# A router product moved from the late turns of a fused two-layer kernel to its first layer, and kept in DRAM in between

## The chip, the core and the metric

The kernel runs on one core of one Trainium2 chip. The metric is the device time of one execution in microseconds (us); lower is better. The engines are named as the profile names them: PE (TensorE, the matrix unit, with PEld for its weight loads), DVE (VectorE), ACT (ScalarE), POOL (GpSimd) and SP (SyncE, which here only issues transfers). SP, ACT and POOL each have a queue of DMA transfers of their own, and all queues feed the same 16 DMA engines.

## What is computed

The input x is 8 sequences of 128 tokens of width 512, all float32. Layer 0 picks one 512x512 matrix for each sequence by an index, multiplies, and puts the result through a small mixture of low-rank experts; the result is added to x. Layer 1 is an attention with 32 query heads and 8 key/value heads over a paged cache of 512 positions and the 128 new ones, followed by a feed-forward part with a router. The change touches only the router of that last part:

```
q      = einsum('bsd,rd->bsr', y, Wq_w)      # Wq_w: 16 x 512
scores = einsum('bsr,er->bse', q, keys)      # keys: 64 x 16
top_w  = softmax(top 16 of 64 scores)
z      = einsum('bsd,nd->bsn', y, A_w)       # 512 -> 64 experts x 8
out    = einsum('bsn,on->bso', z * gate(top_w), B_w) * 2
```

Nothing stands between the two router products, so the kernel multiplies the two weights once, into a matrix of 512 x 64, and then multiplies each y by that matrix. The product of the two weights does not depend on x; it could be made at any time.

## The kernel before, in words

**Layer 0** is the loop at lines 711 to 780, one pass t for each of the 8 sequences. Pass t issues to PE the first half of the sequence's adapter product (`l0_adapter(t, True)`, line 621: 8 multiplications written as 16 instructions, since a float32 product takes two), then pieces of earlier sequences, then the second half (`l0_adapter(t, False)`), which ends with a copy of the result from PSUM to SBUF by ACT (line 630, tile cT). After that come the loads of later sequences on SP's queue, and `l0_base(t)`: the gate product from cT (line 638, tile cp) and the base product from cT and the base weights bww (line 643, tile bp). In pass 0 there is no other sequence to fill the time in which PE waits for the first cT. That is the first wait which the change names. Ahead of the loop PE does 32 transposes of an identity (line 710) while the first loads are under way.

The loads of the start are issued by three queues. ACT's queue has the first input tile and the gate weights. SP's queue has, in this order, the index list, the first sequence's matrix in four pieces of 256 KB (line 510), bww of 1 MB (line 538), the second sequence's input of 256 KB (line 503, tile xT), its matrix of 1 MB (line 510), and then smaller ones. POOL's queue has the norm weights nw (line 118), four pieces of a page list vpg (line 565), the lengths leni (line 579) and the rotation frequencies fr (line 581). POOL issues a transfer by an instruction that keeps it busy for about half a microsecond.

**Layer 1** is a loop of turns u = 1 to 66 (`iteration`), of which 64 are heads of the attention for one sequence. Order on every engine is the order in which the program is written; nothing reorders it later. In a turn PE does the four score products (lines 439 and 442), the output projection of an earlier turn (lines 1062 and 1075, tile y), projections for a later turn (line 265), and the value product (line 938, tile o). The constants read u = NU - 5 = 59 and u = NU - 7 = 57, with NU = 64.

In turn 57 the function `f_weights(0)` takes over a buffer that attention weights have left, and has POOL load the two router weights into it (`fw_t["r"]`, line 817, 16 rows of 2 KB, and `fw_t["k"]`, line 818, 16 rows of 256 bytes) and a part of the first feed-forward weight (line 822). In turn 59, between the second and the third score product, `f_fold` multiplies them: 4 multiplications of 16 x 128 by 16 x 64 (line 828, 8 instructions on PE, tile rk, which the profile calls fr; the frequencies of layer 0 have the same name there, on POOL), and a copy from PSUM into the buffer by DVE (line 831). From turn 59 on, once a turn, `f_project` (line 848) uses the product together with the feed-forward weight, as one matrix of 320 columns.

Two points of the machinery matter below. Each transfer on POOL's queue signals one of 8 semaphores in rotation, and an instruction that issues a transfer first waits until the previous transfer of the same semaphore has landed. And tiles of layer 0 borrow homes in buffers that layer 1 fills later: the matrices of sequences 5 to 7 lie in the first six of the seven slices of the buffer `wo_t`, and slice 6 is empty in layer 0 until `transpose_qk(2, wo_t[:, 6, ...])` writes it at the end of layer 0 (line 794).

Of the kernel before, what the change touches and what calls it, by code (L numbers as in the profile page):

```python
# [9 lines left out]
F32 = mybir.dt.float32  # L10
# [6 lines left out]
P = 128  # L17
B = 8
S = 128
DM = 512  # L20
NC = DM // P
# [18 lines left out]
E1, R1, RD = 64, 8, 16  # L40
# [18 lines left out]
def adaln_ffn_kernel(  # L59
# [25 lines left out]
    nc = tc.nc  # L85
# [33 lines left out]
        out=nw, in_=norm_w.rearrange("o (t d) -> o t d", t=2).to_broadcast([P, 2, D])  # L119
# [16 lines left out]
    yp = ctx.enter_context(tc.tile_pool(name="yp", bufs=2))  # L136
    dram = ctx.enter_context(tc.tile_pool(name="dram", bufs=1, space=bass.MemoryType.DRAM))
    y_d = [dram.tile([P, 4, HN], F32, name=f"yd_{b}") for b in range(B // 2)]
    x1_d = [dram.tile([P, DM], F32, name=f"x1d_{b}") for b in range(B)]
    ya_t, yp_t = {}, {}  # L140

# [7 lines left out]
    wo_t = wp.tile([P, 7, REP * HN], F32, tag="wo", name="wo")  # L149
# [67 lines left out]
    def bank(tag, name):  # L217
        return ps_1.tile([P, DM], F32, tag=tag, name=name)
# [3 lines left out]
    def banks(name, which=None):  # L222
        if which is None:
            which, turn_of[0] = turn_of[0], 1 - turn_of[0]
        return ps_s.tile([P, 2 * DM], F32, tag=f"s{which}", name=name)
# [267 lines left out]
    with ExitStack() as l0:  # L493
# [35 lines left out]
        for b in range(4):  # L529
            t = pairs[b // 2].rearrange("p x n -> p (x n)")[:, b % 2 * NC * DM :][:, : NC * DM]  # L530
            wt_home[b] = t.rearrange("p (o n) -> p o n", o=NC)
        for b in (5, 6, 7):
            t = wo_t[:, 2 * b - 10 : 2 * b - 8].rearrange("p x n -> p (x n)")
# [30 lines left out]
        for i in range(QD):  # L564
            nc.gpsimd.dma_start(
                out=vpg[i * 32 : (i + 1) * 32], in_=vpages[i : i + 1].to_broadcast([32, B * LC])
# [45 lines left out]
        def l0_adapter(b, first):  # L612

            xT, wt, xb = loaded[b]
            if first:
                cp_t[b] = banks(f"cp_{b}", 0)
                lg_t[b] = sm.tile([P, E0 + 8], F32, tag="lg", name=f"lg_{b}")
                nc.gpsimd.memset(lg_t[b][:, E0:], BIG)
            for o in range(0, NC // 2) if first else range(NC // 2, NC):
                for c in range(NC):  # L620
                    nc.tensor.matmul(  # L621
                        out=cp_t[b][:, o * S : (o + 1) * S],
                        lhsT=wt[:, o, c * P : (c + 1) * P],
                        rhs=xT[:, c, :],
                        start=(c == 0),
                        stop=(c == NC - 1),
                    )
            if not first:
                cT_t[b] = p2.tile([P, NC, S], F32, tag="cT", name=f"cT_{b}")
                nc.scalar.copy(cT_t[b].rearrange("p c s -> p (c s)"), cp_t[b][:, :DM])  # L630
# [74 lines left out]
            nc.scalar.copy(half.rearrange("p x c s -> p (x c s)"), tp[:, :DM])  # L705


        idle = bank("q", "idle")
        for i in range(WARM):
            nc.tensor.transpose(idle[:, :S], ident, ident)  # L710
        for t in range(B):
            l0_adapter(t, True)
            if t >= 1:
                l0_turn_low(t - 1)
            if t == 7:
                scores(0, 1, 1)
                mask_exp(0, 1)
                normalize(0, 0)
            l0_adapter(t, False)
            if t + 3 < B:  # L720
                l0_load(t + 3)
            if t + 2 < B:
                l0_load_x(t + 2)
            if t in (3, 4):
                load_q(t - 3)
            if 2 <= t <= 5:
                gather(0, (t - 2) * 4, (t - 1) * 4)
            elif t > 5:
                gather(1, (t - 6) * 8, (t - 5) * 8)
            if t >= 2:  # L730
                l0_turn(t - 2)
            if t == 4:
                project_whole(0, 0, 0, 1)
            if t == 5:
                norms(0)
                make_mask(0)
                project_whole(0, 1, 0, 1)
            if t == 6:
                transpose_qk(0)
                project_whole(0, 0, 1, 1)  # L740
            if t == 7:
                norms(2)
                project_whole(0, 1, 1, 1)
                transpose_qk(1)
            if t >= 1:
                l0_experts(t - 1)
            if t == 7:
                scores(0, 2, 1)
                mask_exp(0, 2)
                normalize(0, 1)  # L750
                new_pb(0)
                blocks(0, 0)
            l0_base(t)
            if t == 0:
                l0_rows()
            if 1 <= t <= 4:
                l0_angles(t - 1)
            if t in (3, 6):
                gather_v(t // 3 - 1, 0, LC)
            if t in (4, 5):  # L760
                make_tables(t - 4)
            if t == 4:
                project_whole(0, 0, 0, 0)
            if t == 5:
                project_whole(0, 1, 0, 0)
                norms(1)
                rotate(0)
                sums_q(nc.gpsimd, 0, 3, 2)
            if t == 6:
                scores(0, 0, 1)  # L770
                mask_exp(0, 0)
                project_whole(0, 0, 1, 0)
                rotate(1)
                sums_q(nc.gpsimd, 0, 4)
            if t == 7:
                scores(0, 3, 1)
                mask_exp(0, 3)
                normalize(0, 2)
                blocks(0, 1)
                project_whole(0, 1, 1, 0)  # L780
# [23 lines left out]
    fw_t, zg_t = {}, {}  # L804

    def f_weights(piece):

        if piece == 0:
            w = wp.tile([P, 7 * 2 * HW], F32, tag="wqkv", name="fw", bufs=GH)
            at = 0  # L810
            for n, rows, c in (("sa", P, NC), ("b", P, NC), ("r", RD, NC), ("k", RD, 1)):
                size = c * {"r": P, "k": E1, "sa": E1 + DM}.get(n, DM)
                fw_t[n] = w[:rows, at : at + size].rearrange("p (c n) -> p c n", c=c)
                at += size
            fw_t["k"] = fw_t["k"][:, 0]
            fw_t["s"], fw_t["a"] = fw_t["sa"][:, :, :E1], fw_t["sa"][:, :, E1:]
            nc.gpsimd.dma_start(out=fw_t["r"], in_=wr.rearrange("r (c p) -> r c p", p=P))
            nc.gpsimd.dma_start(out=fw_t["k"], in_=keys)
        n, c = ("a", piece) if piece < 2 else ("b", piece - 3)
        if piece != 2:  # L820
            src = (aw if n == "a" else bw).rearrange("(c p) n -> p c n", p=P)
            nc.gpsimd.dma_start(out=fw_t[n][:, 2 * c : 2 * c + 2], in_=src[:, 2 * c : 2 * c + 2])

    def f_fold(psum):

        rk = psum("r", [P, NC, E1])
        for c in range(NC):
            nc.tensor.matmul(
                out=rk[:, c, :], lhsT=fw_t["r"][:, c, :], rhs=fw_t["k"], start=True, stop=True
            )  # L830
        nc.vector.tensor_copy(fw_t["s"], rk)

    ORDER = (0, 1, 4, 2, 3, 5, 6, 7)

# [72 lines left out]
    with ExitStack() as l1:  # L907
# [336 lines left out]
        def iteration(u):  # L1244
# [3 lines left out]
            r, group = u % 16, (u // 16 + 1) * GH  # L1248
            f = room(fb) if fb is not None else None

            if u % 4 == 3:
                k, j, four = (u + 5) // 4, 0, True
            elif u % 4 == 0:
                k, j, four = (u + 4) // 4, 0, False
            elif u % 4 == 1:
                k, j, four = (u + 3) // 4, 1, True
            else:
                k, j, four = (u + 2) // 4, 1, False
# [30 lines left out]
            for h in range(REP):  # L1289
                if on(u):  # L1290
                    if (u, h) not in ((1, 0), (1, 1)):
                        scores(u, h)
                        mask_exp(u, h)
                    if h > 0 and (u, h) != (1, 1):
                        normalize(u, h - 1)

                    sums_o(u, h)
                    sums_w(u, h)
                    if 16 <= u < NU - 8 and (r, h) == (2, 3):
                        load_o(u // 16, (1, B12))  # L1300

                    if h == 2:
                        new_pb(u)
                        if u + 2 in range(3, NU):
                            blocks_qk(u + 2, u)
                    if h > 1:
                        blocks(u, h - 2)
                    if h == 1 and u == NU - 5:
                        f_fold(f[1])
                    if h == 3:  # L1310
                        z_blocks(u - NU + 4)
                    if h == (1 if u == NU - 3 else 2) and fb is not None:
                        yT_t[fb] = f_turn(fb, *f)
                if on(u - 3):
                    output(u - 3, h)
                    sums_a(u - 3, h)
                if h > 0 and slots:
                    project(k, j, slots[h - 1 : h])

                if (u, h) in WHOLE:  # L1320
                    project_whole(1, *WHOLE[u, h])
# [23 lines left out]
            if 16 <= u < NU - 8 and r in (0, 1, 2):  # L1345
                n = u // 16
# [184 lines left out]
```

## Time and profile before

| what | value |
|---|---|
| median of 3 runs | 1212.44 us (1210.85 to 1214.88) |
| profiled execution | 1214.63 us, its span 1211.9 us |
| PE busy | 1194.7 us, 99% of the span |
| DVE, POOL, ACT busy | 912.1, 741.2, 504.2 us |
| DMA over the span | 302.71 MB, mean 250 GB/s |
| granted TensorE clock | 1.000 over the span |

The busy time of PE is from the first to the modelled end of each instruction, so 99% says that PE almost never stands without work, not that it works at its peak. The profile's chain of waits is followed back from the last instruction: at each step it goes to what released it, or to the instruction ahead of it on its engine. A piece of work that lies in the chain moves the end if it grows or shrinks; one that does not lie in it moves the end only once it has used up its slack. The granted clock of a stretch is 1.000 when TensorE's clock was not throttled.

### The profile page before, as it was taken

To read this page: it belongs to the slowest core of one execution; us is meant where nothing else is said; L and a number is where in the kernel's file an instruction comes from. 1 tells how busy PE (TensorE), PEld (TensorE's weight loads), DVE (VectorE), ACT (ScalarE), POOL (GpSimd) and SP (SyncE) were. 2 spreads that over 40 slices of the span, in tenths; PEclk is the share of its full clock that TensorE was granted. 3 is DMA by queue.
4 is the path that set the end of the run, shared out by engine and by line. 5 is a ranking of instruction groups with operands and counts; after the bars stand their busy time and mean duration, and the time that the engine had idled before them with its cause. 6 is when DMAs were issued, how large, how long until landed. Compare 5 with 4: busy or idle time off the path is not lost.

```text
span 1211.9 us, 16793 instructions
## 1 busy us (share of the span) xinstructions
PE 1194.7 (99%) x4159; PEld 714.1 (59%) x4159; DVE 912.1 (75%) x2103; ACT 504.2 (42%) x1457; POOL 741.2 (61%) x826
## 2 busy tenths in 40 slices
PE   8999899999999999999999999999999999999998
PEld 6666455565555656555556555555656555565554
DVE  3547788877987887888887787878878888877632
ACT  1244554444444444444444444444444444443211
POOL 2444689778755677578756685687657684743100
PEclk9999999999999999999999999999999999999999
DMA  8823788888888988888889978897989888887742
GB/s 310 269 93 107 237 249 247 254 272 282 258 256 249 313 250 271 260 290 287 244 256 284 289 231 281 288 290 239 276 248 305 255 262 249 269 269 232 232 140 96
DMA packets 206260, 302.71 MB, mean 250 GB/s; under 512 B 84755, under 2 KB 119828, under 8 KB 205268
## 3 DMA queue, kind: packets, MB, share of 16 engines
q1 hardware_dynamic: 171220, 197.02, 53.4%
q10 hardware_dynamic: 18720, 52.49, 13.8%
q0 software_dynamic: 16224, 52.14, 12.5%
q8 instruction: 33, 0.54, 0.2%
q14 instruction: 63, 0.52, 0.1%
HBM read 185.64 MB, written 115.93 MB: 249 GB/s over the span
## 4 chain that ended last, share of the span: by engine, by line
PE 89%; DMA 5%; issue 1%; DVE 1%; POOL 1%; ACT 1%; ACTq 0%; SPq 0%; DVEq 0%; POOLq 0%
PE o L938 20%; PE p L265 19%; PE s L439 17%; PE y L1062 13%; PE s L442 4%; PE p L298 3%; DMA px<-pb 3%; PE y L1075 2%; PE bp L643 2%; PE op L1418 2%; PE cp L621 2%; PE fr L848 1%; PE fz L848 1%; DMA qkb<-px 1%; DMA bww<-in_base_w 1%
## 5 line engine op out<-in xcount | busy, mean ns | idle before, releaser
L463 ACT ACTIVATE p<-p,low 128x640 f32<-128x640 f32 x256 | 211.8, 827 | 438.3 <-DVE den L468 270.8
L469 POOL TENSOR_SCALAR p<-p,den 128x640 f32<-128x640 f32 x256 | 210.8, 824 | 230.1 <-DVE den L468 228.8
L452 DVE CUSTOM_DVE_ANT_0 p<-s,mask,rs 128x640 f32<-128x640 f32 x256 | 222.1, 878 | 80.7 <-PE s L442 80.0
L265 PE MATMUL p<-wqkv,xo 128*128 128x384 f32 x784 | 280.7, 486 | 0.4 <-POOL wqkv L166 0.3
L439 PE MATMUL s<-kt,qkT 128*128 128x512 f32 x504 | 258.4, 594 | 4.9 <-ACT oT L961 2.2
L938 PE MATMUL o<-pT,vt 128*128 128x512 f32 x512 | 230.2, 592 | 0.0
L474 DVE STREAM_TRANSPOSE pb<-p 128x640 f32<-128x640 f32 x252 | 208.0, 826 | 23.7 <-POOL p L469 23.7
L1062 PE MATMUL y<-wo,oT 128*128 128x256 f32 x784 | 206.4, 380 | 0.0
L265 PEld LDWEIGHTS p<-wqkv,xo 128*128 128x128 f32 x784 | 148.4, 190 | 69.1 <-POOL wqkv L166 1.2
L442 PEld LDWEIGHTS s<-qkT 128*128 128x128 f32 x504 | 95.8, 190 | 120.5 <-issue 120.5
L206 POOL DMA_INDIRECT vt<-in_vc,vrow x128 | 138.8, 1084 | 40.9 <-issue 31.1
L938 PEld LDWEIGHTS o<-pT,vt 128*128 128x128 f32 x512 | 97.2, 190 | 107.9 <-issue 92.8
L439 PEld LDWEIGHTS s<-kt,qkT 128*128 128x128 f32 x504 | 94.3, 190 | 77.8 <-issue 30.3
L1062 PEld LDWEIGHTS y<-wo,oT 128*128 128x128 f32 x784 | 131.8, 191 | 8.7
L314 ACT ACTIVATE sq<-c 128x128 f32<-128x128 f32 x320 | 98.8, 309 | 8.1
L442 PE MATMUL s<-qkT 128*128 128x128 f32 x504 | 96.8, 274 | 0.0
L320 POOL TENSOR_TENSOR rs<-ss,mhalf 128x5 f32<-128x5 f32 x64 | 83.1, 1299 | 5.3
L961 ACT COPY oT<-o 128x512 f32<-128x512 f32 x64 | 37.5, 585 | 100.7 <-PE o L938 73.0
L318 POOL TENSOR_SCALAR ss<-ss,eps 128x5 f32<-128x5 f32 x64 | 26.5, 414 | 77.4 <-ACT sq L314 77.3
L938 PE MATMUL o<-pT,vn 128*128 128x512 f32 x128 | 65.4, 592 | 0.0
L425 DVE STREAM_TRANSPOSE pb<-ca 128x640 f32<-128x640 f32 x61 | 50.9, 835 | 18.0 <-DMA kt<-in_kc 10.5
L268 DVE TENSOR_TENSOR c<-c,p 128x384 f32<-128x384 f32 x84 | 44.9, 534 | 21.7 <-PE p L265 21.4
(194 smaller groups left out, 1435.5 us busy)
## 6 DMA issues: line engine op xcount, KB each, us to landing
pT<-px SPq DMA_DIRECT2D x64, 1280.0 KB, 7.6
px<-pb SPq DMA_DIRECT2D x122, 400.0 KB, 5.4
px<-pb ACTq DMA_DIRECT2D x122, 400.0 KB, 5.6
qkb<-px SPq DMA_DIRECT2D x61, 320.0 KB, 4.3
kt<-in_kc SPq DMA_DIRECT2D x512, 32.0 KB, 4.9
wqkv<-in_wqkv POOLq DMA_DIRECT2D x32, 384.0 KB, 4.7
wo<-in_wo POOLq DMA_DIRECT2D x17, 512.0 KB, 8.1
yd<-yp POOLq DMA_DIRECT2D x12, 512.0 KB, 9.3
```

The source lines that it names most:

```text
L206: nc.gpsimd.indirect_dma_start(out=kv_t[step][1][:, c, :], out_offset=None, in_=vc, in_offset=bass.IndirectOffsetOnAxis(ap=vrow[:, hf, at ...
L265: nc.tensor.matmul(out=ps, lhsT=xo[:, pr, x, c, :], rhs=w[:, c, :], start=(c == 0), stop=(c == 1))
L314: nc.scalar.activation(sq, cs[:, at : at + D], AF.Square, accum_out=ss[:, h : h + 1])
L320: nc.gpsimd.tensor_tensor(rs, ss, mhalf, ALU.pow)
L439: nc.tensor.matmul(out=s[:, :L], lhsT=qkT[:, h, :], rhs=kt[:, :, g % GH, :], start=True, stop=True)
L442: nc.tensor.matmul(out=s[:, L:NK], lhsT=qkT[:, h, :], rhs=qkT[:, REP, :], start=True, stop=True)
L452: nc.vector.tensor_tensor_reduce(out=p, in0=s_t.pop((u, h))[:, :NK], in1=mask_t[st], scale=rs_t[u][:, h : h + 1], scalar=BIG, op0=ALU.add, ...
L463: nc.scalar.activation(p, p, AF.Exp, bias=low, scale=-1.0, accum_out=den)
L469: nc.gpsimd.tensor_scalar(p_t[u, h], p_t[u, h], den, 1.0, ALU.mult, ALU.mult)
L474: nc.vector.transpose(pb_t[u][:, :, h * w : (h + 1) * w].rearrange("p i (j a) -> p j i a", a=32), p_t.pop((u, h)).rearrange("p (j i a) -> ...
L938: nc.tensor.matmul(out=o, lhsT=vt[:, c, j * D : (j + 1) * D] if c < LC else vn_t.pop(u), rhs=pT[:, c], start=(c == 0), stop=(c == LC),)
L1062: nc.tensor.matmul(out=y_t["y"][:, half * HN : (half + 1) * HN], lhsT=part(key)[:, i * S : (i + 1) * S], rhs=wo_t[:, slot(w, key[0] // (B ...
```

## The change

The product of the two router weights is made in pass 0 of layer 0, in the wait for the first cT, and written to a new DRAM tile `fold_d` (128 x 4 x 64 floats, 128 KB). In turn 57 `fold_d` is loaded in place of the two weights, and in turn 59 DVE copies it to its place beside the feed-forward weight; the four multiplications of turn 59 are gone. The two weights are loaded at the start into the empty slice 6 of `wo_t`, by two more transfers at the end of POOL's first group, after fr.

```diff
+    fold_d = dram.tile([P, NC, E1], F32, name="fold_d")
...
+        fr_w = wo_t[:RD, 6, :DM].rearrange("r (c p) -> r c p", c=NC)
+        fk_w = wo_t[:RD, 6, DM : DM + E1]
+        fold = wo_t[:, 6, DM + E1 :][:, : NC * E1].rearrange("p (c n) -> p c n", c=NC)
+        nc.gpsimd.dma_start(out=fr_w, in_=wr.rearrange("r (c p) -> r c p", p=P))
+        nc.gpsimd.dma_start(out=fk_w, in_=keys)
+
+        def l0_fold():
+            rk = bank("kv", "rk")[:, : NC * E1].rearrange("p (c n) -> p c n", c=NC)
+            for c in range(NC):
+                nc.tensor.matmul(
+                    out=rk[:, c, :], lhsT=fr_w[:, c, :], rhs=fk_w, start=True, stop=True
+                )
+            nc.vector.tensor_copy(fold, rk)
+            nc.gpsimd.dma_start(out=fold_d, in_=fold)
...
             l0_adapter(t, False)
+            if t == 0:
+                l0_fold()
             if t + 3 < B:
                 l0_load(t + 3)
...
-            fw_t["k"] = fw_t["k"][:, 0]
+            for n, width in (("sa", E1 + DM), ("b", DM), ("f", E1)):
+                fw_t[n] = w[:, at : at + NC * width].rearrange("p (c n) -> p c n", c=NC)
+                at += NC * width
...
-            nc.gpsimd.dma_start(out=fw_t["r"], in_=wr.rearrange("r (c p) -> r c p", p=P))
-            nc.gpsimd.dma_start(out=fw_t["k"], in_=keys)
+            nc.gpsimd.dma_start(out=fw_t["f"], in_=fold_d)
...
-    def f_fold(psum):
-
-        rk = psum("r", [P, NC, E1])
-        for c in range(NC):
-            nc.tensor.matmul(
-                out=rk[:, c, :], lhsT=fw_t["r"][:, c, :], rhs=fw_t["k"], start=True, stop=True
-            )
-        nc.vector.tensor_copy(fw_t["s"], rk)
+    def f_fold():
+
+        nc.vector.tensor_copy(fw_t["s"], fw_t["f"])
...
-                        f_fold(f[1])
+                        f_fold()
```

More of the change, by code (lines that the diff above doesn't have):

```diff
@@ L810, in f_weights @@
             at = 0
[L811 to L814, printed above, removed]
-            fw_t["k"] = fw_t["k"][:, 0]
+            for n, width in (("sa", E1 + DM), ("b", DM), ("f", E1)):
+                fw_t[n] = w[:, at : at + NC * width].rearrange("p (c n) -> p c n", c=NC)
+                at += NC * width
             fw_t["s"], fw_t["a"] = fw_t["sa"][:, :, :E1], fw_t["sa"][:, :, E1:]
-            nc.gpsimd.dma_start(out=fw_t["r"], in_=wr.rearrange("r (c p) -> r c p", p=P))
-            nc.gpsimd.dma_start(out=fw_t["k"], in_=keys)
+            nc.gpsimd.dma_start(out=fw_t["f"], in_=fold_d)
         n, c = ("a", piece) if piece < 2 else ("b", piece - 3)
```

## The prediction

> **What bounds the kernel now.** I read the page's busy line first: PE is busy 1194.7 us of 1211.9, so I look for what the change takes from PE and adds to it. Then the chain of waits, in the two places that the change touches. Its pieces are start, length, engine and line. In turn 59:
>
> ```profile
> 1062.03 0.22 PE s L442 x2
> 1062.25 1.03 PE fr L828 x8
> 1063.28 1.06 PE y L1062 x4
> ...
> 1065.85 0.86 PE y L1062 x4
> ```
>
> The fold's eight instructions lie in the chain with 1.03 us, and the output product behind them takes 1.06 instead of the 0.86 that the same form takes two rows on. Nothing but PE stands in the chain from there to the end, apart from 0.59 us of an ACT copy at 1147.5 that PE itself starts, and the last 0.42 us on DVE. So work taken from PE here moves the end.
>
> At the start the chain is another:
>
> ```profile
> 4.67 9.10 DMA bww<-in_base_w
> 13.77 0.04 issue
> 13.81 3.70 PE bp L643 x8
> 17.51 1.78 PE cp L621 x16
> ```
>
> The end waits for the base weights until 13.77, then for PE. What PE does ahead of that is in the timeline (start, length, engine, line; in brackets the idle time before, and what ended it):
>
> ```profile
> 10.39 1.16 PE L621 MATMUL cp<-xT,wqkv 128*128 128x128 f32 x8 [0.32 <-DMA wqkv<-in_w]
> 11.59 0.59 ACT L630 COPY cT<-cp 128x512 f32<-128x512 f32 x1 [8.66 <-PE cp L621]
> ...
> 12.23 1.19 PE L638 MATMUL cp<-glw,cT 128*128 128x136 f32 x8 [0.68 <-ACT cT L630]
> ...
> 13.81 1.12 PE L643 MATMUL bp<-bww,cT 128*128 128x512 f32 x2 [0.39 <-DMA bww<-in_base_w]
> ```
>
> Here is the wait that the change fills, 11.55 to 12.23, and a second one of 0.39 us, for bww, which also counts as room.
>
> **What goes.** Turn 59 loses eight instructions of PE: 1.03 us, and the 1.06 - 0.86 = 0.20 us that the switch back costs. **-1.23 us**, all of it in the chain. What is late next there? DVE stands idle 1.72 us before its next score row at 1065.45, and the probabilities of the last turn are sent for at 1148.67 and used by PE at 1163.89, so neither takes the gain back. The DVE copy (0.42 us) stays, from SBUF now, behind the same row; that DVE idles 1.72 us hides it. In turn 57 POOL loses two issues (0.58 and 0.52 us) and gains one of 128 rows of 1 KB. The row of that shape is nw's, 0.74 us, so POOL is 0.36 us earlier at its next row, a normalization that DVE waited 0.23 us for; PE has no idle time there. Cost of both: nothing. The load of 128 KB has two turns to land, where the neighbouring 512 KB took 3.9 us.
>
> **What comes, apart from the wait.** On PE 1.03 us plus some part of the 0.20: I take 1.1 us. The DVE copy of 0.42 lies in a stretch where DVE idles 7.55 us. POOL's write of `fold_d` waits for that copy; behind it on POOL is the bias sum of line 672, which before starts at 19.13, when its own load lands. The write is issued well ahead of it (below: about 17.5 plus 0.74), so it costs nothing, and 1 us more would still find later sums with time to spare (DVE uses the first one at 22.16). If both weights were in SBUF at 11.55, the fold would run from there to 12.65, the gate product 1.0 us (the chain has 1.01 and 0.93 for it in passes 1 and 2) to 13.65, and bww would still be last at 13.77. Then the start costs nothing.
>
> **Are the weights there?** That decides the case. The two transfers are the eighth and ninth of POOL's queue. PE's first fold instruction waits for both. Before, POOL issues leni at 5.17 and fr at 5.73, free at 6.29; with 0.58 and 0.52 us for the new ones (turn 57's rows) they are issued at 6.3 and 6.9. The ninth reuses nw's semaphore, whose load lands at 5.7, so that wait is free. How long do they fly? In the list of DMA issues (KB of each, median us to landing):
>
> ```profile
> nw<-in_norm_w POOLq DMA_DIRECT2D x1, 128.0 KB, 4.2
> vpg<-in_vpages POOLq DMA_DIRECT2D x4, 4.0 KB, 4.9
> fr<-in_inv_freq POOLq DMA_DIRECT2D x1, 32.0 KB, 7.5
> fw<-in_wr POOLq DMA_DIRECT2D x1, 32.0 KB, 3.6
> ...
> leni<-in_lens POOLq DMA_DIRECT2D x1, 4.0 KB, 6.7
> ...
> fw<-in_keys POOLq DMA_DIRECT2D x1, 4.0 KB, 3.2
> ```
>
> nw lands at 1.53 + 4.2 = 5.73, leni at 5.17 + 6.7 = 11.87, fr at 5.73 + 7.5 = 13.23. Size is not what counts (leni is 4 KB): the queue moves on by (13.23 - 5.73) / 6 = **1.25 us for each transfer**, while the DMA engines carry SP's megabytes. wr and keys come behind fr: 13.23 + 2 x 1.25 = 15.73. The bounds: in turn 57 wr and keys themselves land 3.6 and 3.2 us after their issues at 1037.40 and 1037.97, so at 1041.0 and 1041.2, 0.2 us apart, which gives 13.23 + 0.4 = 13.6; and if they fall behind the second sequence's matrix, for which SP's queue waits until 17.01, about 17.4. I take 15.73, by the six rows of the same queue in the same stretch.
>
> [...]
>
> **The sum.** PE starts the fold at 15.73 + 0.04 (the step from bww's landing to bp), 1.1 for the fold, 1.0 for the gate product: bp at 17.87 instead of 13.81, **+4.06 us**. bww has long landed, and the next sequence's matrix too (17.0, needed at 21.4). Everything behind bp in the chain is PE, or waits of 0.75 to 1.1 us that PE's own results end, so the delay goes through. Net +4.06 - 1.23 = **+2.83 us**. The profiled execution would go from 1214.63 (its span 1211.9 and 2.7 around it) to 1217.5. It lies 2.2 us above the median, so on the median: **1215.3 us**, +0.23%. A measurement of this kernel can tell about 0.3% (3.6 us) from no change; the three runs of before lie 4.0 us apart. So the forecast is "within 0.3%", on the slow side.
>
> **Rivals.**
>
> *The wait is hidden, and the kernel gains.* If the two transfers land by about 11.7, or by the time that the two waits allow, the result is -1.23: 1211.2. For it: one packet per DMA engine each, little to move. Against it: fr, ahead of them in the same queue, lands at 13.23. Chance 0.08. A bunched landing (13.6 to 14.8) is between: +0.7 to +1.9, chance 0.19.
>
> *Slower by more than 0.3%: the weights fall behind the megabyte.* Place: the DMA engines from 14.4 on, where the input of sequence 1 is through (5.15 + 9.3 = 14.45) and its matrix has them until 17.0. Price: landing at 17.4, bp at 19.54, +5.73 - 1.23 = +4.5: 1216.9. It decides once keys lands after 16.5 (0.04 + 1.1 + 1.0 - 13.81 - 1.23 + 16.5 = 3.6). For it: keys is last of nine, and all of its 16 shares have to be in; the slowest decides. Against it: POOL's queue got a turn about once in 1.25 us throughout.
>
> Added to either: *PE's clock.* PE would stand idle from 11.55 to 15.8, 4.2 us, where the longest idle stretch of the trace is 1.88 us. The first transposes show what a throttled start costs: by the table of stretches 15 of them fill 3.13 us before 4.5, and 19 fill 1.80 us after 4.6. If the clock falls in the gap, about 3.2 us of work at half pace lose 1.6 us: forecast +4.4 (1216.9), with the late landing +6.1 (1218.5), at worst twice the 1.6. (The clock column reads 1.00 in both stretches; the pace tells it, not the column.) After the 1.88 us of idle the short score product, at 140.45, has its usual 0.38 us, so it takes more than that. [...] I give late landing and fallen clock together 0.33.
>
> *The change does not do what it says.* The compiled order has the fold behind the adapter's last product and ahead of the gate product, as written, and turn 59 without its eight instructions; so no chance for that. 0.02 is left for a gain over 0.3% that I can't name.
>
> **How the numbers follow.** Forecast case (landing 14.8 to 16.5, clock kept): 0.38, 1215.3. Bunched 0.19, hidden 0.08, late or throttled 0.33, other 0.02. Faster by over 0.3%: 0.02, and 0.01 for the scatter of the runs. Slower by over 0.3%: the 0.33 and 0.03 of the forecast case's upper end. Same: the rest, 0.61. The range leaves out the hidden case and the worst of the late ones: low 1211.7, high 1219.0.
>
> **What would show it.** In the changed profile: the two loads at about 6.3 and 6.9 with 8 to 9 us to landing; PE waiting 3 to 5 us for wo (their tile) before the fold; bp at 17 to 19 instead of 13.81, now released by PE; turn 59 without line 828, and the product behind it at 0.86; the chain from 18 on shifted as a whole. The forecast fails if keys lands before 12, if the instructions behind the fold show double lengths (clock), or if some later transfer takes the shift up.

## The result and the profile after

The changed kernel has a median of **1218.93 us** (1211.57 to 1224.64, 22 runs) against 1214.97 us of the kernel before on the same chip (1209.98 to 1223.40, 22 runs): ratio **1.0032, 95% interval 1.0019 to 1.0045**. In a second set of runs, on a chip shared with two experiments below, it was 1218.61 against 1213.73 us: 1.0043, 1.0028 to 1.0059. So the change costs 4 to 5 us where the forecast had 2.83 us, and lies just beyond the 0.3% that the forecast called no change. The forecast time was 1215.3 us; the result is just below the upper end of its range, 1219.0.

The profiled execution of the changed kernel took 1214.63 us (span 1212.9), by chance the same as the one of before. Two single executions can't show a difference of 4 us in the total; they can show where each stage was moved. This execution lies 4.3 us below the median of its kernel. At the start, the chain of waits (start, length, engine, line) answers to the rows 4.67 to 17.51 of before:

```profile
6.29 0.48 POOL wo L712
6.77 7.35 DMA wo<-in_keys
14.12 0.04 issue
14.16 1.10 PE rk L718 x8
15.26 1.12 PE cp L639 x8
16.38 5.13 PE bp L644 x8
21.51 1.78 PE cp L622 x16
...
27.06 3.43 PE bp L644 x8
```

The last line is the base product of pass 1, which the chain of before has at 23.06:

```profile
23.06 3.43 PE bp L643 x8
```

The chain no longer comes through bww but through POOL's issues and the transfer of keys, 4 KB that take 7.35 us to land at 14.12. Then PE makes the product (1.10 us), the gate product (1.12) and the base product, and here is the second thing to see: bp has 5.13 us, where it had 3.70 before. In the timeline (in brackets the idle time before, and what ended it) PE stood idle ahead of the product for 2.81 us:

```profile
14.16 1.10 PE L718 MATMUL rk<-wo 16*128 16x64 f32 x8 [2.81 <-DMA wo<-in_keys]
...
16.22 5.29 PE L644 MATMUL bp<-bww,cT 128*128 128x512 f32 x8
```

The table of stretches tells why bp is long. Its columns are the stretch, its length, busy time of PE, PEld, DVE, ACT and POOL (with instructions), the granted clock, the DMA share and GB/s. First the kernel before:

```profile
12.00:17.00 5.00, 4.38 (x16) 2.43 (x16) 2.70 (x19) 0.47 (x2) 0.00 (x0) 1.00 0.99 397
17.00:22.00 5.00, 5.00 (x38) 4.19 (x37) 0.00 (x0) 0.85 (x2) 1.31 (x2) 1.00 1.04 410
```

Then the changed kernel:

```profile
12.00:17.00 5.00, 2.84 (x17) 2.27 (x18) 0.86 (x4) 0.00 (x0) 0.60 (x1) 0.93 1.01 402
17.00:22.00 5.00, 5.00 (x14) 2.49 (x13) 2.27 (x17) 0.30 (x1) 1.31 (x2) 0.73 1.04 410
22.00:60.00 38.00, 35.43 (x206) 25.58 (x205) 18.10 (x64) 8.22 (x18) 14.67 (x21) 1.00 0.71 246
```

The granted clock is 0.93 and 0.73, where before has 1.00 in both stretches: the trace's clock records (its list of when the clock was granted in full or in part) have half pace from 16.29 for 3.41 us. PE was full from 17 to 22 and finished 14 instructions, before 38.

In turn 59 the chain is now

```profile
1064.16 0.22 PE s L443 x2
1064.38 0.87 PE y L1072 x4
1065.25 0.86 PE s L440 x2
```

The eight instructions are gone, and the output product behind the scores has 0.87 us instead of 1.06. DVE's copy there got longer. The same 128x256 floats were copied out of PSUM before and are copied from SBUF to SBUF now:

```profile
L831 DVE COPY fw<-fr x1: 425/425/425, 1063.3 to 1063.3; 128x256 f32<-128x256 f32 x1
```

```profile
1065.31 1.50 DVE L841 COPY fw<-fw 128x256 f32<-128x256 f32 x1
```

The first line, of the kernel before, has 425 ns; the second, of the changed kernel, 1.50 us. In this trace PE loses nothing by it.

A sum by places, each the start of the same PE instruction in both traces: the first bp +2.41 us (13.81 to 16.22), the bp of pass 1 +4.00, the last value product ahead of the place where turn 59 had its eight instructions +2.14, the next one +0.91. The last step is the -1.23 us of turn 59. Between pass 1 and turn 59 the difference wanders (+3.9, +5.7, +2.1) with gaps of 0.3 to 2 us at PE that differ from execution to execution, in the kernel before as well.

### The profile page after: what moved, and what is told of

Read it like the earlier page. It is cut to its first block, busy times and chain, and to the rows that moved or that the text cites. A ratio compares the mean times of both kernels' runs of the same rounds, so it can differ in the third digit from the quotient of the medians.

```text
span 1212.9 us, 16798 instructions
## 1 busy us (share of the span) xinstructions
PE 1196.6 (99%) x4159; PEld 715.9 (59%) x4159; DVE 913.4 (75%) x2104; ACT 504.1 (42%) x1457; POOL 740.1 (61%) x828
## 4 chain that ended last, share of the span: by engine, by line
PE 90%; DMA 3%; POOL 2%; DVE 1%; issue 1%; ACT 1%; SPq 1%; ACTq 0%; DVEq 0%; POOLq 0%
PE o L948 20%; PE p L266 19%; PE s L440 17%; PE y L1072 13%; PE s L443 4%; PE p L299 3%; PE bp L644 2%; PE y L1085 2%; PE op L1428 2%; PE cp L622 2%; PE fr L858 1%; DMA kt<-in_kc 1%; PE fz L858 1%; PE cp L639 1%; DMA px<-pb 1%
```

## The experiments

The theory after the result: the loss is (a) PE's wait for keys, with the product and the gate product behind it, about +2.4 us, and (b) the clock that falls in or after that wait, some +1.7 us for a fall of 3.41 us as in the trace above; turn 59 gives 1.23 back. Rivals: the loss is the wait alone; the late part (the load of 128 KB in turn 57, the copy) costs something, or doesn't gain; the new DRAM tile or POOL's write costs something wherever it stands. In all eleven runs the kernel before ran beside them on the same chip (29 to 35 runs against 12). The edits are shown against the changed kernel, that of y2 against the kernel before; "..." stands for lines left out. The clock lost by an execution is worked out as (1 - granted clock) x span, and given as a mean over the runs; the clock of a run is on record to 0.001, which is 1.2 us.

**x1_act_queue.** The two early loads go to ACT's queue, right behind the gate weights.

```diff
...
+        nc.scalar.dma_start(out=fr_w, in_=wr.rearrange("r (c p) -> r c p", p=P))
+        nc.scalar.dma_start(out=fk_w, in_=keys)
...
-        nc.gpsimd.dma_start(out=fr_w, in_=wr.rearrange("r (c p) -> r c p", p=P))
-        nc.gpsimd.dma_start(out=fk_w, in_=keys)
```

> The changed kernel with its two early loads moved from the end of POOL's first group to ACT's queue, right behind the gate weights; all else as changed. Theory (the loss is the wait for the weights on POOL's queue, plus the throttled clock that the idle stretch causes): the weights land before 8 us, PE runs the fold from about 11.4, base product at 13.8 to 13.9 as before the change, clock 1.000; against before -1.2 us (0.999). Rival (the loss comes from having the fold in this place at all, or from the later round trip through DRAM): the base product starts late or the time stays at about +3.9 us (1.003).

Measured: 1215.49 against 1214.03 us, ratio 1.0012 (0.9994 to 1.0030). The chain at the start:

```profile
4.66 9.51 DMA bww<-in_base_w
14.16 0.04 issue
14.21 3.70 PE bp L649 x8
17.91 1.78 PE cp L627 x16
```

In the timeline of PE the product and the gate product stand ahead of that, without a wait:

```profile
11.31 1.10 PE L718 MATMUL rk<-wo 16*128 16x64 f32 x8
12.34 1.19 PE L644 MATMUL cp<-glw,cT 128*128 128x136 f32 x8
14.21 3.70 PE L649 MATMUL bp<-bww,cT 128*128 128x512 f32 x8 [0.67 <-DMA bww<-in_base_w]
```

The chain comes through bww again, bp has its 3.70 us, and it starts 0.40 us later than before, because bww lands at 14.16 instead of 13.77. So it was POOL's queue that made the weights late, and without that the product is hidden and, in this trace, the clock kept (1.000 over the span). The 1.2 us that the expectation hoped to gain did not come by time: 0.9990 lies just outside the interval. A price of two more transfers among the first ones would explain some of it but isn't shown: in the six traces with no added transfer at the start (before, y1, y2, y3, w1, w2) bww lands anywhere from 13.47 to 14.56, and 14.16 is within that. The mean clock lost is 1.52 us against 0.87 of the kernel before.

**x2_filled.** PE is kept busy through the wait by 22 transposes of the identity ahead of the product.

```diff
         def l0_fold():
+            warm = bank("q", "warm")
+            for i in range(22):
+                nc.tensor.transpose(warm[:, :S], ident, ident)
```

> The changed kernel with 22 idle transposes of 0.11 us (2.4 us of work that nobody uses) ahead of the fold, so that PE is busy while it waits for the weights. Theory (part of the loss is the clock that falls because PE idles): the wait stays, bp starts at about 16.2 as in the changed kernel, but its eight products keep 0.43 us each and the granted clock is 1.000; against before +1.2 us, some 2 to 3 us better than the changed kernel. Rival (the clock has other reasons, for instance the sixteen-row products): bp still shows 0.85 us for some products, clock 0.997 to 0.999, time as the changed kernel, +3.9 us.

Measured: 1215.64 against 1214.03 us, 1.0012 (1.0000 to 1.0025). In the chain:

```profile
11.90 2.40 PE warm L718 x22
14.30 1.03 PE rk L721 x8
15.33 1.12 PE cp L639 x8
16.45 3.43 PE bp L644 x8
```

The product stands where it stood (14.30 against 14.16), bp starts 2.48 us later than in the kernel before, but takes 3.43 us and not 5.13, and pass 1 is late by 2.37 us instead of 4.00. The clock was kept through the start (1.00 in each stretch up to 60 us); over its whole span this execution, the longest of its set with 1218.97 us, has 0.997. With this work that computes nothing in the wait the mean clock lost is 1.21 us against 2.93 of the changed kernel, and 0.997 or less stands in 1 of 12 runs against 23 of 34. The time goes the same way: x3 (next), which has the changed start without the transposes and ran on the same chip, is 3.6 us slower, of which 1.23 are turn 59; by time alone the rest isn't clear of the intervals. This separates (a) from (b): the wait alone, less turn 59, is 2.4 - 1.23 = 1.2 us, and 1.6 was measured (the interval holds 0 to 3.0).

**x3_start_alone.** The early part stays; turns 57 and 59 are as before, so that the product is made twice and the early one isn't used.

```diff
-            nc.gpsimd.dma_start(out=fw_t["f"], in_=fold_d)
+            nc.gpsimd.dma_start(out=fw_t["r"], in_=wr.rearrange("r (c p) -> r c p", p=P))
+            nc.gpsimd.dma_start(out=fw_t["k"], in_=keys)
...
-                        f_fold()
+                        f_fold(f[1])
```

> The start of the changed kernel (loads, fold and write to DRAM in layer 0) together with turns 57 and 59 as before, so that the product is made twice; the early one is not used. Theory: turn 59 is worth 1.23 us, so this is 1.2 us slower than the changed kernel, about +5.1 us (1.004) against before, and the chain in turn 59 shows 1.03 and 1.06 us again. Rival (the late part of the change gave nothing, or cost): the time equals the changed kernel's +3.9 us or is less.

Measured: 1219.23 against 1214.03 us, 1.0040 (1.0025 to 1.0055). The whole loss is in the early part. In the timeline of PE the clock falls earlier and for twice as long:

```profile
14.44 1.60 PE L718 MATMUL rk<-wo 16*128 16x64 f32 x8 [2.94 <-DMA wo<-in_keys]
15.98 2.18 PE L639 MATMUL cp<-glw,cT 128*128 128x136 f32 x8
17.95 5.46 PE L644 MATMUL bp<-bww,cT 128*128 128x512 f32 x8
```

The granted clock is 0.79 from 12 to 17 and 0.53 from 17 to 22, together 6.8 us at half pace, from 14.9 on; the product, the gate product and bp are all long, and pass 1 is 5.90 us late. Against the two results of the changed kernel, 1.0032 and 1.0043, the missing gain of turn 59 doesn't show in the times; it is a tenth of a per cent, and the intervals are 0.26% to 0.31% wide.

**x4_pass3.** The product goes behind the base product of pass 3; loads as in the change.

```diff
-            if t == 0:
-                l0_fold()
...
             l0_base(t)
+            if t == 3:
+                l0_fold()
```

> The changed kernel with the fold behind the base product of pass 3 instead of in pass 0, where PE idles 1.10 us at 47.2 in the trace of before and the weights have long landed; loads as changed. Theory: no wait at the start, bp of pass 0 at 13.8, clock 1.000, the fold's 1.03 us inside the idle 1.10 us, so -1.0 to -1.2 us against before (0.999). Rival (two more transfers on POOL's queue cost by themselves, by delaying the base weights): bp of pass 0 is later than 13.8 though nothing waits for the new loads, and the time is above before.

Measured: 1214.33 against 1214.03 us, 1.0007 (0.9992 to 1.0022). The gain of 1.0 to 1.2 us that was expected doesn't show by time here either. The first bp is 0.30 us late (bww lands at 14.07, again within the spread of the starts without added transfers), turn 59 gains its 1.23 us (the difference to before goes from +2.52 to +1.29 there). The mean clock lost is 1.11 us.

**y1_late_alone.** The late part alone: nothing is made at the start, and turn 57 loads 128 KB of the base weights in place of the product.

```diff
...
-            nc.gpsimd.dma_start(out=fw_t["f"], in_=fold_d)
+            nc.gpsimd.dma_start(out=fw_t["f"], in_=base_w.rearrange("(p r) n -> p r n", p=P)[:, 0, : NC * E1].rearrange("p (c n) -> p c n", c=NC))
```

> Turns 57 and 59 as in the changed kernel, layer 0 as before: no early loads, no early fold, no DRAM tile; turn 57 loads 128 KB of a weight of layer 0 in place of the product, so the product is left out and only the time counts. It asks what the late part is worth by itself, since the fold without its wait (in pass 3, or with loads on ACT's queue) has not shown the gain of 1.23 us. Theory (the late part gains 1.23 us and the missing gain lies in the start or in the scatter): -1.2 us (0.999). Rival (the load or the copy of 128 KB in the late turns costs as much as the fold did): the same as before or above.

Measured: 1214.74 against 1213.60 us, 1.0002 (0.9987 to 1.0017), where -1.23 us would be 0.9990. The trace has the gain: the difference to before goes from +3.58 to +2.36 in turn 59. The interval holds both answers, so it was run again (w2 below).

**y2_hole.** The kernel before, with the DRAM tile `fold_d` in the same place and one write of 256 bytes into it by POOL in pass 3.

```diff
+    fold_d = dram.tile([P, NC, E1], F32, name="fold_d")
...
+            if t == 3:
+                nc.gpsimd.dma_start(out=fold_d[:1, 0, :], in_=ident[:1, :E1])
```

> The kernel before, with the DRAM tile of 128 KB put where the change puts it, so that all later DRAM tiles move by 128 KB, and one transfer of 256 bytes into it in pass 3; nothing else. Theory (where DRAM tiles lie does not matter): same as before, 1.000. Rival (the shift of the exchange buffers costs something all along): +1 to +2 us (1.001 to 1.0015).

Measured: 1213.99 against 1213.60 us, 1.0007 (0.9990 to 1.0024). The first bp is 0.05 us off; no cost of the tile shows.

**y3_pass3_clean.** x4 with the two loads issued by POOL in pass 1, at about 26 us, so that nothing is added to the first transfers.

```diff
-        nc.gpsimd.dma_start(out=fr_w, in_=wr.rearrange("r (c p) -> r c p", p=P))
-        nc.gpsimd.dma_start(out=fk_w, in_=keys)
...
-            if t == 0:
-                l0_fold()
...
+            if t == 1:
+                nc.gpsimd.dma_start(out=fr_w, in_=wr.rearrange("r (c p) -> r c p", p=P))
+                nc.gpsimd.dma_start(out=fk_w, in_=keys)
+            if t == 3:
+                l0_fold()
```

> The changed kernel with the fold in pass 3 and its two loads issued by POOL in pass 1, at about 26 us, where the DMA engines are free of the first loads. Theory: the base weights land at 13.8 as before, nothing is added to the start, the idle 1.1 us of pass 3 hides the fold: -1.2 us (0.999). Rival (something else in the change costs 1 to 2 us, wherever the fold stands): 1.000 to 1.001.

Measured: 1212.91 against 1213.60 us, **0.9985 (0.9973 to 0.9998)**. In the timeline of PE at pass 3:

```profile
43.67 3.60 PE L644 MATMUL bp<-bww,cT 128*128 128x512 f32 x8
47.20 1.10 PE L716 MATMUL rk<-wo 16*128 16x64 f32 x8
48.23 2.05 PE L622 MATMUL cp<-xT,wt 128*128 128x128 f32 x16
```

The kernel before has a wait of 1.10 us in this place, ahead of the product `cp<-xT,wt`:

```profile
43.63 3.60 PE L643 MATMUL bp<-bww,cT 128*128 128x512 f32 x8
48.32 2.02 PE L621 MATMUL cp<-xT,wt 128*128 128x128 f32 x16 [1.10 <-issue]
```

The router product fits into it exactly: the next work starts at 48.23, the first bp is at -0.01 us and the first value product of layer 1 at -0.04. This is the hidden product that the change was after, in another wait.

**y4_pool_front.** The two loads stay on POOL's queue but move forward, right behind nw.

```diff
...
+        nc.gpsimd.dma_start(out=fr_w, in_=wr.rearrange("r (c p) -> r c p", p=P))
+        nc.gpsimd.dma_start(out=fk_w, in_=keys)
...
-        nc.gpsimd.dma_start(out=fr_w, in_=wr.rearrange("r (c p) -> r c p", p=P))
-        nc.gpsimd.dma_start(out=fk_w, in_=keys)
```

> The changed kernel with the two early loads moved four places forward in POOL's queue, right behind nw's; fold in pass 0 as changed. It tests the claim that the place in the queue sets the landing: theory, each place is worth 1.0 to 1.3 us, so they land at about 7 and 8.3 (second and third of the queue in the trace of before), ahead of the fold at 11.3; no idle stretch, bp at 13.8 to 14.2 and the clock kept there; against before -1.2 to -0.8 us. Rival (it is the first packets of these two loads, or their issue, that is slow): keys lands at 12 or later, and PE waits as in the changed kernel.

Measured: 1214.91 against 1213.60 us, 0.9997 (0.9982 to 1.0011). Its PE timeline:

```profile
12.09 1.10 PE L718 MATMUL rk<-wo 16*128 16x64 f32 x8
13.12 1.19 PE L644 MATMUL cp<-glw,cT 128*128 128x136 f32 x8
15.09 5.40 PE L649 MATMUL bp<-bww,cT 128*128 128x512 f32 x8 [0.78 <-DMA bww<-in_base_w]
```

The two loads take 5.4 us each, and the product waits for nothing. So a place further forward in the queue ends the wait; keys lands 5.2 us earlier, at 8.95, of which 3.2 us are the earlier issue (3.58 instead of 6.77) and 2.0 the shorter flight. But bww now lands at 15.05 (10.39 us after its issue, before 9.10), later than in any start without added transfers, bp is 1.28 us late, and in this execution the clock fell at 15.3 after a gap of 0.78 us (granted 0.83 from 12 to 17 and from 17 to 22): pass 1 is 2.98 us late. Whether bww is as late in the other runs isn't on record; their mean clock lost, 1.21 us, is that of x2.

**w1_pass3_again, w2_late_again, w3_after_again.** The kernels of y3 and y1 and the changed kernel again, on one chip.

> The kernel of y3_pass3_clean a second time, on whichever chip is given, to see whether its gain stands. If the product costs PE 1.1 us in pass 3 with no wait and gives back 1.23 us in turn 59, the two cancel and the ratio to the kernel before is 1.000 (within 0.001); if y3's 0.9985 was real, about 0.9985 again, which the instructions of PE alone can't explain.

> The kernel of y1_late_alone a second time (the product is left out, turn 57 loads 128 KB of the base weights in its place). By turn 59 alone 1.23 us less than the kernel before, ratio 0.999; if the load of 128 KB or its place in turn 57 costs something that takes the gain up, 1.000 or more, as the first run's 1.0002 had it.

> The changed kernel itself, beside the two others on the same chip. If the wait of about 2.4 us at the start and the falls of the clock behind it cause the loss, it is 3 to 4 us above the kernel before again (1.0025 to 1.0035), its mean clock lower than that of the other two by 0.001 to 0.002; if the 1.0032 belonged to one chip, nearer to 1.001.

Measured against 1213.73 us: w1 1212.45, 0.9993 (0.9976 to 1.0010); w2 1212.53, 0.9991 (0.9972 to 1.0010); w3 1218.61, 1.0043 (1.0028 to 1.0059). The changed kernel is slower again, by 4.9 us, and 6 us behind the same product in pass 3. In its second trace keys lands earlier and the clock falls earlier, so that it is the gate product and the start of bp that are long:

```profile
6.75 6.40 DMA wo<-in_keys
13.15 0.04 issue
13.20 1.10 PE rk L718 x8
14.30 1.96 PE cp L639 x8
16.26 4.28 PE bp L644 x8
```

For w1 the working in the expectation was wrong: the product does not cost 1.1 us in pass 3, it fills the 1.10 us wait, so that turn 59's 1.23 us should remain, a ratio of 0.9990. The two results, 0.9985 and 0.9993, lie about it, as do 1.0002 and 0.9991 of the late part alone. (In w1's trace the product fits into the wait of pass 3 as in y3, but bww lands at 14.56 and the first bp is 0.79 us late, though nothing was added to the start.) Over the seven sets that drop the product of turn 59 and have no wait for keys (x1, x4, y1, y3, y4, w1, w2) the ratios average 0.9998. That the version with the product in pass 3 is faster than the kernel before rests on its traces and on one interval of two; that it is faster than the changed kernel is shown.

One thing in the late part is left. In all ten traces that copy from SBUF in turn 59 DVE needs 1.50 us for it, and in w1 the chain of waits runs through it:

```profile
1064.52 1.42 DVE fw L842
1065.94 0.79 DVE p L453
```

In each of the ten, turn 59 gains its 1.23 us, read at the next value product; by the value product after that, six of them (y3, x4, y4, w1, x2, x1) have lost 0.2 to 0.8 us of it, and the other four, both traces of the changed kernel among them, nothing. In x3 and y2, which copy from PSUM as before, the difference does not move there. So the gain of the late part is 1.23 us at most, and the copy is what may take some of it back; outside w1 that isn't shown.

That the clock is the other part of the loss shows over all runs, in their granted clocks: 0.997 or less in 23 of 34 runs of the changed kernel, and in 3 of the 99 runs of the kernel before that have their clock on record. Within the changed kernel the time goes with the clock: the two runs at 1.000 average 1214.2 us, the eight at 0.999 1216.6, and the 21 at 0.997 1219.7. The mean clock lost is 2.93 and 2.94 us in the two sets of the changed kernel, 2.23 in x3, 0.51 to 1.52 in the other nine sets, and 0.67 to 0.90 in the three sets of the kernel before.

## Why the prediction was right, and where it was not

*What goes.* -1.23 us in turn 59, in the chain: all traces that drop the eight instructions have it, and those of x3 and y2, which keep them there, don't. This term was exact, and in both traces of the changed kernel nothing takes it back, as said; in six other traces something does, by 0.2 to 0.8 us. By time alone the gain isn't resolved.

*The queue.* That the weights wouldn't be there, because they are the last two of POOL's queue under SP's megabytes, was right, and x1 shows it: on another queue there is no wait. The term that was mis-sized is the landing. "wr and keys come behind fr: 13.23 + 2 x 1.25 = 15.73" took the queue's mean progress for every transfer. In the two traces that have all three landings, wr came 0.34 and 0.40 us behind fr and keys 0.19 behind wr (x3: 13.87, 14.21, 14.40; x4: 13.26, 13.66, 13.85), as its lower bound from turn 57 had it. Keys landed at 14.12, 14.40 and 13.15 in the three traces of this start (the changed kernel, x3, w3). The first two are the bunched landing of 13.6 to 14.8, for which 0.19 was given, the third is earlier still. Bp came at 16.22, not 17.87: +2.41 instead of +4.06 us.

*The clock.* The forecast case had "clock kept", and this is the step that failed. The gap that PE stood idle was 2.81 us, shorter than the 4.2 foreseen, and the clock fell all the same: in the changed kernel at 16.3, in x3 at 14.9, and in w3 during the gate product, which has 1.96 us instead of 1.12. The three gaps of this start are 2.81, 2.94 and 2.32 us. The price of one fall was well worked out ("lose 1.6 us"; 4.00 - 2.41 = 1.59), but it was left to a rival, and how likely a fall was in such a gap was the author's estimate, which no trace of before shows.

*The sum.* +4.06 forecast and +4.00 found at pass 1: a wait too long by 1.65 us stood in for a fall of the clock of 1.59. The net of +2.83 was thus near by luck, two errors that cancel, and it is the sum of one execution with one fall. The three traces of this start come apart in the same way. From the landing of keys to bp it is 2.10 us at full clock (14.12 to 16.22), so that the landings at 14.12, 13.15 and 14.40 alone make bp 2.41, 1.44 and 2.69 us late; the rest of the delay at pass 1 (4.00, 3.02 and 5.90 us) is the clock, 1.59, 1.58 and, with the 6.8 us at half pace, 3.21. Over the runs the clock loss is 2.0 to 2.3 us above that of the kernel before, more than one fall: 2.2 for the wait (mean of the three traces), +2.1 for the clock, -1.23, makes +3.1 us. Measured are +4.0 and +4.9 by the medians. The sum is within the first interval (2.3 to 5.5 us) and just outside the second (3.4 to 7.2); what the difference is stays open. The start of x3 would give 5.90 - 1.23 = +4.7, and a run at 0.997 has lost about as much clock as two falls of 3.41 us; such starts may thus be the common ones, but only the traces tell where in a run the clock fell.

*The chances.* "Within 0.3%" had 0.61, and the result is 0.32% and 0.43%. The 0.33 for a late landing or a fallen clock was too small: the forecast case itself had a gap of 4.2 us in it, and yet 0.38 with the clock kept.

*The covers.* POOL's write, DVE's copy in pass 0 and the load in turn 57 cost nothing that shows, as said; y2 and w2 agree. The copy in turn 59 was mis-sized: "The DVE copy (0.42 us) stays, from SBUF now", but it takes 1.50 us in every trace; why it is longer isn't shown. It costs PE nothing in the two traces of the changed kernel. That the two loads could delay others was not in the forecast: bww landed at 14.16 in x1, 14.07 in x4 and 15.05 in y4, against 13.77 before, but only y4's lies beyond the 13.47 to 14.56 of the starts without them. In the changed kernel bww lies behind the wait for keys.

## What to carry to other kernels

A wait on the tensor engine is room only if the operands of the work put into it are already there: read the landing times of the queue's neighbours under load, and not the size of the transfer (keys, 4 KB, took 7.35 us). Price a new gap twice, for its length and for the clock that may fall in it (here 2.2 and 2.1 us, by the sum above), and look for a wait later in the program, when the first transfers are through; here a wait of 1.10 us in pass 3 took the same product, and in its two traces that cost nothing. When the landing can't be helped, idle work on the tensor engine can be cheaper than the gap, as in x2, where pass 1 was late by 2.37 us instead of 4.00.

## What the runs showed of the hardware

The clock fell after gaps of 2.81, 2.94 and 2.32 us in the three traces of the changed start, and not always after the same gap. In the kernel before, the changed kernel and w1 PE waits 1.88 or 1.89 us ahead of a score product at about 140 us. In the first two the clock held there (1.00 from 138 to 146); in w1 this is the timeline of PE:

```profile
135.61 2.75 PE L299 MATMUL p<-wqkv,xo 128*128 128x384 f32 x8
140.24 1.49 PE L440 MATMUL s<-kt,wo 128*128 128x512 f32 x2 [1.88 <-DVE low L453]
141.52 0.64 PE L443 MATMUL s<-wo 128*128 128x128 f32 x2
141.94 3.91 PE L299 MATMUL p<-wqkv,xo 128*128 128x384 f32 x8
```

The short score product takes 0.64 us where the two others have 0.38, and the same eight projections take 3.91 us instead of 2.75. The prediction had concluded from the one trace of before that "it takes more than that"; one execution can't exclude it. In y4 a gap of 0.78 us, behind the product of 1.10 us with its 16 rows, was followed by a fall; x1 has the same product and a gap of 0.67 us and held its clock (1.000 over the span), and so did x4 with a gap of 0.93 us and no such product ahead of it (1.000). What sets these apart isn't shown.

The transfer of keys, 4 KB on POOL's queue, took 6.4 to 7.6 us to land where it was the last of nine in the first 15 us, 5.4 us where it was moved ahead of six others, and 3.2 us in turn 57. The four pieces of the page list, 4 KB each and ahead of it in the same queue, have a median of 4.9 us in the kernel before. With one size the time went from 3.2 to 7.6 us; the 5.4 us are those of y4, which changes only the place of the two loads in the queue.

The landing of a 1 MB transfer in the first 15 us moves by itself: bww came at 13.47 to 14.56 in six traces whose queues have the same first transfers, two of them of one kernel (13.76 in y3, 14.56 in w1). A delay of 0.3 or 0.4 us in one trace is therefore no evidence of a cause.

A copy of 128x256 floats by DVE took 0.42 us out of PSUM and 1.50 us from SBUF to SBUF in turn 59, the same in all ten traces that have it.
